# Layer 3's feed-forward block: the parts of a finished sequence move to other places in the software pipeline

## The chip, the cores and the metric

The program runs on one core of a Trainium2 chip. The metric is the device time of one execution in microseconds, the median of several runs. A core has five engines with a queue of instructions each: TensorE (PE; its weight loads are listed apart as PEld), VectorE (DVE), ScalarE (ACT), GpSimd (POOL) and SyncE (SP, which issues transfers). An engine works through its queue in order; semaphores make it wait for the others.

## What is computed

The kernel is a network of four layers, each a feed-forward block, an attention block and the same feed-forward block again, with residuals. The change lies in layer 3's feed-forward block, which is called twice (before and after layer 3's attention). It is itself a small transformer of two inner layers over 4 sequences of 512 tokens, 128 features wide:

```python
def _layer(x, wqkv, qs, ksc, wo, lg, lb, w1, b1, w2, b2):
    h = shift_token(x)                # half of the features come from the token before
    q, k, v = split(h @ wqkv)         # 8 heads of 64
    q, k = rotary_xpos(l2norm(q) * qs, l2norm(k) * ksc)
    o = local_attention(q, k, v)      # windows of 64, each sees itself and the one before
    x = x + o @ wo
    h = shift_token(x)
    h = (h - mean(h)) / sqrt(var(h) + 1e-05) * lg + lb
    a, g = split(h @ w1 + b1)
    return x + (a * gelu(g)) @ w2 + b2
```

Everything is float32.

## The kernel before

`l3_ffn` handles eight **units**: a unit is one inner layer of one sequence, units 0 to 3 are the first inner layer of the four sequences and 4 to 7 the second. A unit is four **steps** of 128 tokens, so a call has 32 steps. `yT` holds the sequences with features on partitions.

The loop over `n` is a software pipeline with a hand-written order. In one turn of the loop it issues six stages, each for another step, in six places:

- place 0, `project` (step n): PE multiplies the shifted tokens by the weights of q and k (`p_qk`) and of v (`pv`). ACT squares q and k (`sq`, line 1737) and copies `v`; DVE multiplies by the rotary tables (`t`, lines 1791 and 1794) and sums the squares (`rn`, 1796); POOL makes the inverse roots of the norms with ten small operations (`ir`, lines 220 to 230), adds the rotary halves (line 1798) and scales k (line 1799). SyncE moves two halves of `v` into `vb`.
- place 1, `to_features` (step n-2): PE transposes q and k (`pt_qk`), ACT copies q (`qT`), DVE copies k (`kT`, line 1823).
- place 2, `exponentials` (step n-4): eight exponentials on ACT with row sums (`s`, line 1737), the reciprocal of the sums on DVE (`sm`, 1860) and the scaling of the weights on POOL (`s<-s,sm`, 1861).
- place 3, `weights` (step n-3): scores on PE (`ps`), mask and maximum on DVE (`s`, 1844; `nm`, 1846 and 1849).
- place 4, `turn_weights` (step n-5): eight transposes of the weights on PE (`pt`), copied by ACT (`PT`).
- place 5, `with_values` (step n-6): PE's products with the values (`po`), copied by DVE (`oT`, line 1887).

When a unit's four steps are through, its feed-forward part is cut into **parts**, and a table `parts` gives each a turn of the loop (counted from the unit's first step) and a place. A part is issued just ahead of the stage in that place:

- `attended` (10, 2): output projection `pz` on PE, the residual sum `yT` on DVE (line 1903), then the shifted copy `h2` (shown as `h` in the profile): ACT copies 64 partitions as they are (line 1740) and DVE the other 64 moved by one token (line 1755)
- `mean` (10, 4): a product with ones gives the mean (`pm`, PE), DVE subtracts it (line 1912), ACT squares the result (`sq2`, shown as `sq<-h`)
- `variance` (11, 0): `pvar` on PE, `rs` on DVE (line 1923), and its inverse root on POOL (lines 214 and 215; 215 is a power)
- `spread` (11, 4): a diagonal of the inverse roots, `dg`, on DVE (line 1931)
- `normed` (12, 0): PE spreads `dg` over the partitions (`pb`), DVE multiplies `h2` by it (line 1941)
- `hidden` 0 (12, 5), 1 and 2 (13, 0): two products each (`pag`), a gelu on ACT (`ge`), and on DVE the product of both (`hh`, line 1954)
- `close_unit` (13, 4): `pz2` on PE, the sum into `yT` on DVE (line 1966)
- `leave` (14, 0), second inner layer only: transposes `pt_z`, the residual, and the output's store or the next normalisation

Three things set the order on the engines. What PE and ACT are given through `mm_in_order`, `transpose_in_order`, `act` and `act_copy` stays in the order in which the program issues it. DVE and POOL are ordered by the scheduler of the framework, by its own estimate. And PSUM has eight banks: three pairs (tag `d`: `p_qk`, `pt_qk`, `ps`, `pt`, `pag`) and two single ones (tag `m`: `pv`, `po`, `pz`, `pm`, `pvar`, `pb`, `pz2`, `pt_z`), each taken in turn, so that a group of products waits until the tile three pairs (or two banks) earlier has been read.

The last unit of a call doesn't go by the table: its parts follow the loop in the list `rest` (in the first call they are spread over the attention that follows).

Of the kernel before, what the change touches and what calls it, by code (L numbers as in the profile page):

```python
# [115 lines left out]
def tile_macaron(ctx, tc, x_in, const_in, vec_in, w0_in, ws_in, ws3_in, w2f_in, w3_in, out):  # L116
# [17 lines left out]
    def bank(tag, name):  # L134
        n = 2 if tag == "d" else 1
        return psum["pool"].tile([P, n * 512], F32, tag=tag, name=name, bufs=psum["bufs"][tag])

    def two_banks(name):

        if "d" in psum["bufs"]:  # L140
            p = bank("d", name)
            return p[:, 0:512], p[:, 512:1024]
        return [bank("e" if "e" in psum["bufs"] else "q", name) for _ in range(2)]
# [3 lines left out]
    for b in range(B):  # L147
        nc.sync.dma_start(x[:, ts(b, TB), :], x_in[:, ts(b, TB), :])
        if b == 0:
            a, z = W0.at["ip"]  # L150
# [24 lines left out]
    yT = keep.tile([P, B, S], F32, name="yT")  # L175
# [8 lines left out]
    def mm_in_order(dst, lhsT, rhs, start=True, stop=True):  # L184
        tc.keep_in_program_order(nc.tensor.matmul(dst, lhsT=lhsT, rhs=rhs, start=start, stop=stop))  # L185

    def transpose_in_order(dst, src):
        tc.keep_in_program_order(transpose(dst, src))
# [107 lines left out]
    def chain(b):  # L296
        parts = deque()
        chains.append([b, clock[0], parts])
        return lambda gap, f, products=True: parts.append((gap, f, products))
# [14 lines left out]
    def leave_normed(b, spare, gap, pinned=False, start=1, to_route=True):  # L314

        st = []
        spare(start, lambda: st.append(statistics(x, b)), False)

        def scale():
            scaled(y, x, b, st[0], pinned)  # L320
            ready.add(b)

        spare(1, scale, False)
        spare(gap, lambda: turn(b))
        if routed and to_route:
            spare(1, lambda: logits(b))
            if b % 2:
                first, second, third = route(b // 2)
                spare(1, first, False)
                spare(routed["gaps"][0], second)  # L330
                spare(routed["gaps"][1], third)
# [1391 lines left out]
    def l3_ffn(w3, tag, first, rb):  # L1723
        with pool(tag) as sb, banks(tag + "ps", d=3, m=2):
            units = [(l, b) for l in range(2) for b in range(B)]
            n_steps = TB * len(units)
            u_state = {}
            s_state = {}

            def W(l, name):  # L1730
                return W3(w3, f"{name}{l}")

            def tmp(name):
                return rb.tile([P, S], F32, tag="tmp", name=name, bufs=4)

            def act(*args, **kw):
                tc.keep_in_program_order(nc.scalar.activation(*args, **kw))  # L1737

            def act_copy(dst, src):
                tc.keep_in_program_order(nc.scalar.copy(dst, src))  # L1740
# [4 lines left out]
            def light(u):  # L1745

                return nc.gpsimd if u else nc.vector

            def shift(dst, src, at=slice(0, S), u=1):

                act_copy(dst[0:64, at], src[0:64, at])
                a = max(at.start, 1)
                if at.start == 0:
                    light(u).memset(dst[64:128, 0:1], 0.0)
                nc.vector.tensor_copy(dst[64:128, a : at.stop], src[64:128, a - 1 : at.stop - 1])
# [134 lines left out]

            whole = slice(0, S)

            def attended(u, at=whole):
                l, b = units[u]
                oT = u_state[u]["oT"]
                n = at.stop - at.start
                pz = bank("m", "pz")
                for fc in range(4):
                    mm_in_order(
                        pz[:, :n], W(l, "wo").rearrange("p (c n) -> p c n", n=D)[:, fc, :], oT[:, fc, at], fc == 0, fc == 3  # L1900
                    )
                z = yT[:, b, :]
                nc.vector.tensor_add(z[:, at], pz[:, :n], z[:, at])
                if at.start == 0:
                    u_state[u]["h2"] = rb.tile([P, S], F32, tag="h2", name="h2", bufs=2)
                shift(u_state[u]["h2"], z, at)

            def mean(u, at=whole):
                h2, n = u_state[u]["h2"], at.stop - at.start
                pm = bank("m", "pm")  # L1910
                mm_in_order(pm[:, :n], onesm, h2[:, at])
                nc.vector.tensor_sub(h2[:, at], h2[:, at], pm[:, :n])
                sq = u_state[u]["sq", at.start] = tmp("sq2")
                act(sq[:, :n], h2[:, at], AF.Square)

            def variance(u, at=whole):

                sq, n = u_state[u].pop(("sq", at.start)), (at.stop - at.start) // P
                pv = bank("m", "pvar")
                for t in range(n):  # L1920
                    mm_in_order(pv[:, 2 * t : 2 * t + 2], sq[:, ts(t, P)], onesm[:, 0:2])
                rs = u_state[u]["rs", at.start] = rb.tile([P, TB], F32, tag="rs", name="rs", bufs=2)
                nc.vector.tensor_copy(rs[:, :n], pv[:, : 2 * n].rearrange("p (t i) -> p t i", i=2)[:, :, 0])
                eng = nc.vector if u == len(units) - 1 else nc.gpsimd
                inverse_root(rb, rs[:, :n], rs[:, :n], f"ir{n}", ALU.add, 1e-5, eng)
# [17 lines left out]
            def hidden(u, c, at=whole):  # L1943
                l, b = units[u]
                a, n = HCH[c]
                h2, w1, m = u_state[u]["h2"][:, at], W(l, "w1"), at.stop - at.start
                if c == 0 and at.start == 0:
                    u_state[u]["hh"] = rb.tile([P, 3, S], F32, tag="hh", name="hh")
                pg, pa = two_banks("pag")
                mm_in_order(pg[:n, :m], w1[:, HID + a : HID + a + n], h2)  # L1950
                mm_in_order(pa[:n, :m], w1[:, a : a + n], h2)
                ge = tmp("ge")
                act(ge[:n, :m], pg[:n, :m], AF.Gelu, bias=W(l, "b1g")[:n, c : c + 1])
                nc.vector.scalar_tensor_tensor(
                    u_state[u]["hh"][:n, c, at], pa[:n, :m], W(l, "b1a")[:n, c : c + 1], ge[:n, :m], ALU.add, ALU.mult
                )
# [13 lines left out]
            def leave(b, at=whole):  # L1970
                pt = bank("m", "pt_z")
                t0, n = at.start // P, (at.stop - at.start) // P
                for t in range(n):
                    transpose_in_order(pt[:, ts(t, P)], yT[:, b, ts(t0 + t, P)])
                tiles = slice(b * TB + t0, b * TB + t0 + n)
                xb = x[:, tiles, :].rearrange("p t d -> p (t d)")
                nc.vector.scalar_tensor_tensor(xb, pt[:, : n * P], 0.5, xb, ALU.mult, ALU.add)
                if first:
                    leave_normed(b, chain(b), 3)
                else:  # L1980
                    nc.sync.dma_start(out[:, tiles, :], x[:, tiles, :])
# [17 lines left out]
            if first:  # L1999
                scale_layer(0)  # L2000

            parts = [
                (attended, 10, 2), (mean, 10, 4), (variance, 11, 0), (spread, 11, 4), (normed, 12, 0),
                (lambda u: hidden(u, 0), 12, 5), (lambda u: hidden(u, 1), 13, 0), (lambda u: hidden(u, 2), 13, 0),
                (close_unit, 13, 4), (lambda u: leave(units[u][1]) if units[u][0] else None, 14, 0),
            ]
            later, last = {}, len(units) - 1
            for u in range(len(units)):
# [6 lines left out]
            for n in range(-2, n_steps + 6):  # L2015
                for place, (part, lag) in enumerate((
# [6 lines left out]
                    tick()  # L2023
            assert not later, later
            rest = [attended, mean, variance, spread, normed]
            rest += [lambda u, at, c=c: hidden(u, c, at) for c in range(3)] + [close_unit, lambda u, at: leave(units[u][1], at)]
            if first:
# [13 lines left out]
    with pool("ws") as wp:  # L2041
# [9 lines left out]
        with pool("l2x") as l2x:  # L2051
# [58 lines left out]
            with pool("l2g") as sb, banks("l2gps", a=2, g=2, t=2, m=2):  # L2110
# [7 lines left out]
                while slots:  # L2118
                    n = slots[0][0]
                    run_to(slots, n)  # L2120
                    at = (n - SLOTS - 1) * part
# [12 lines left out]
    with pool("l3r") as rb:  # L2134
        l3_ffn(w3, "l3f", True, rb)
        l3_attn()
        l3_ffn(w3, "l3g", False, rb)
# [145 lines left out]
```

## Time and profile before

| | us |
|---|---|
| median of 3 runs | 2669.72 (2664.33 to 2672.69) |
| profiled execution | 2684.83 |
| its span | 2683.0 |
| first call of `l3_ffn`, loop | about 1529.7 to 1935 |
| second call of `l3_ffn` | about 2264 to 2683 |

| engine | busy us | share of the span |
|---|---|---|
| PE | 2274.4 | 85% |
| DVE | 1776.3 | 66% |
| ACT | 1306.2 | 49% |
| POOL | 951.7 | 35% |

Shares over the whole span mix many stages; the change is judged within the two calls. Three views serve there. The table of windows gives the busy time of each engine in a stretch, with the clock that PE was granted (1.00 is full speed). The table of waits adds up an engine's idle time by the instruction that waited and the one that released it. The timeline lists instructions in order of time, with the idle time of the engine ahead of each. A step can be cut out of the timeline by `sq<-p_qk`, ACT's square of the projections, which comes once in each step.

### The profile page before, as it was taken

What the parts mean: (1) busy time and instruction counts of PE and PEld (TensorE: products, weight loads), DVE (VectorE), ACT (ScalarE), POOL (GpSimd) and SP (SyncE); (2) the same over time, 40 slices, a digit from 0 to 9 for tenths busy, and PEclk for the clock granted to TensorE, in tenths of its full rate; (3) what the DMA queues carried; (4) which work ended last, traced back from release to release, by engine and by line L of the source; (5) the groups of instructions that cost most, each with busy time, mean ns of one, the idle gap of its engine ahead of it and who ended that gap; (6) DMA issues with size and microseconds to landing.
All of it is one profiled execution on the core that took longest, in us unless ns stands there. A gap on an engine that the chain in (4) does not pass through costs nothing.

```text
span 2683.0 us, 50819 instructions
## 1 busy us (share of the span) xinstructions
PE 2274.4 (85%) x19070; PEld 1288.0 (48%) x19070; DVE 1776.3 (66%) x4790; ACT 1306.2 (49%) x3159; POOL 951.7 (35%) x1532
## 2 busy tenths in 40 slices
PE   6578589988679989988787778998899998799988
PEld 2255244443344434477567645555433333555555
DVE  3745667775676777565554488777567775877774
ACT  3056125443333544343443357776525554677773
POOL 2023023232232233214331377766310001876761
PEclk8789799998889999789778879999989999899998
DMA  3052000000000000246145701010000000110100
GB/s 146 8 175 73 0 1 2 1 1 1 1 1 1 1 5 1 84 146 216 32 139 160 246 23 23 21 23 19 1 1 1 1 1 9 27 23 19 23 21 13
DMA packets 40142, 113.21 MB, mean 42 GB/s; under 512 B 7064, under 2 KB 16536, under 8 KB 39384
## 3 DMA queue, kind: packets, MB, share of 16 engines
q1 hardware_dynamic: 36520, 100.94, 11.8%
q0 software_dynamic: 2944, 6.04, 1.1%
q8 instruction: 151, 2.47, 0.4%
q10 hardware_dynamic: 432, 2.98, 0.3%
q14 instruction: 95, 0.78, 0.1%
HBM read 79.78 MB, written 15.47 MB: 35 GB/s over the span
## 4 chain that ended last, share of the span: by engine, by line
PE 56%; DVE 21%; ACT 8%; POOL 8%; issue 5%; DMA 1%; another core or an unknown queue 0%; POOLq 0%; DVEq 0%; SPq 0%; ACTq 0%
PE pk_at L185 10%; PE po_at L185 6%; PE pa L185 4%; PE pq_at L185 4%; PE pag L185 4%; PE po L185 3%; ACT s L1737 3%; PE pg L185 2%; PE pe L185 2%; PE p_qk L185 2%; DVE t L1794 2%; DVE t L1791 2%; PE pz L185 2%; PE idle L185 2%; PE pt L182 2%
## 5 line engine op out<-in xcount | busy, mean ns | idle before, releaser
L894 ACT ACTIVATE PT<-pk_at 128x512 f32<-128x512 f32 (+3 forms) x768 | 335.3, 488 | 401.2 <-PE pq_at L185 254.0
L185 PE MATMUL pk_at<-qx,km 32*128 32x512 f32 (+3 forms) x1536 | 401.4, 555 | 5.9 <-ACT PT L894 2.7
L866 DVE CUSTOM_DVE_ANT_0 s<-pq_at,cst 128x384 f32<-128x384 f32 (+3 forms) x512 | 249.9, 488 | 99.0 <-PE pq_at L185 44.8
L185 PE MATMUL pq_at<-km,qT 32*128 32x128 f32 (+3 forms) x1024 | 275.8, 504 | 18.3 <-DVE nm L866 14.4
L1737 ACT ACTIVATE s<-s,nm,rn 128x128 f32<-128x128 f32 x512 | 245.5, 482 | 3.2 <-DVE nm L1849 3.0
L897 POOL TENSOR_SCALAR_AFFINE_SELECT PT<-PT 128x256 f32<-128x256 f32 x256 | 104.5, 410 | 381.7 <-ACT PT L894 381.6
L185 PEld LDWEIGHTS pk_at<-qx,km 32*128 32x128 f32 x1536 | 147.1, 190 | 154.3 <-issue 93.5
L185 PE MATMUL po_at<-PT,vh 128*32 128x128 f32 (+3 forms) x2432 | 205.6, 395 | 8.7 <-POOL PT L897 6.9
L868 DVE TENSOR_REDUCE nm<-pq_at 128x1 f32<-128x512 f32 x256 | 165.4, 685 | 55.3 <-PE pq_at L185 53.8
L1798 POOL TENSOR_TENSOR t<-t,t 128x1024 f32<-128x1024 f32 x64 | 151.2, 2362 | 109.7 <-DVE t L1794 105.1
L215 POOL TENSOR_TENSOR ln_r<-ir,minus_half 128x4 f32<-128x4 f32 x60 | 62.0, 1034 | 351.5 <-DVE ir L214 349.5
L185 PE MATMUL pq_at<-km,t 32*128 32x512 f32 x512 | 170.9, 661 | 0.7 <-DVE nm L868 0.4
L185 PE MATMUL p_qk<-w,hT 128*128 128x512 f32 x256 | 142.4, 684 | 15.6 <-DVE t L1794 9.6
L1861 POOL TENSOR_TENSOR s<-s,sm 128x1024 f32<-128x1024 f32 x64 | 121.3, 1896 | 52.1 <-DVE sm L1860 44.1
L185 PEld LDWEIGHTS po_at<-PT,vh 128*32 128x32 f32 x2432 | 54.4, 109 | 174.4 <-issue 128.5
L182 PE MATMUL pt<-ident,s 128*128 128x128 f32 x640 | 94.0, 295 | 48.5 <-POOL s L1861 32.0
L185 PEld LDWEIGHTS pq_at<-km,qT 32*128 32x128 f32 x1024 | 110.6, 191 | 48.9 <-DVE nm L866 28.9
L1419 POOL DMA_INDIRECT xg<-yd,come x60 | 57.5, 958 | 180.3 <-PE pt_x L182 72.3
L289 ACT COPY yT<-pt_y 128x512 f32<-128x512 f32 x56 | 32.7, 584 | 180.0 <-PE pt_y L182 179.5
L1737 ACT ACTIVATE sq<-p_qk 128x1024 f32<-128x1024 f32 x64 | 65.5, 1023 | 109.8 <-PE p_qk L185 61.6
L182 PEld LDWEIGHTS pt<-ident,s 128*128 128x128 f32 x640 | 79.0, 151 | 81.1 <-POOL s L1861 44.2
L1791 DVE TENSOR_TENSOR t<-p_qk,w 128x1024 f32<-128x1024 f32 x64 | 78.3, 1223 | 58.5 <-ACT sq L1737 53.0
(457 smaller groups left out, 5374.7 us busy)
## 6 DMA issues: line engine op xcount, KB each, us to landing
wf<-in_w2f_dram SPq DMA_DIRECT2D x45, 836.0 KB
vb<-v SPq DMA_DIRECT2D x112, 128.0 KB
w<-in_w2f_dram SPq DMA_DIRECT2D x15, 836.0 KB
skew<-qe SPq DMA_DIRECT2D x16, 512.0 KB
rel<-skew SPq DMA_DIRECT2D x64, 128.0 KB
od<-o SPq DMA_DIRECT2D x60, 64.0 KB
w<-in_w_dram SPq DMA_DIRECT2D x1, 3200.0 KB
w<-in_w_dram SPq DMA_DIRECT2D x12, 173.0 KB
```

Source lines behind the costliest of these rows:

```text
L182: return nc.tensor.transpose(dst, src, ident[: src.shape[0], : src.shape[0]])
L185: tc.keep_in_program_order(nc.tensor.matmul(dst, lhsT=lhsT, rhs=rhs, start=start, stop=stop))
L215: nc.gpsimd.tensor_tensor(dst, v, minus_half[:, :n], ALU.pow)
L866: nc.vector.tensor_tensor_reduce(s[:, :nk], pq[:, :nk], causal[:, S - nk :], 1.0, -BIG, ALU.add, ALU.max, to)
L868: nc.vector.tensor_reduce(to, pq, AX.X, ALU.max)
L894: by_order(nc.scalar.activation(PT[:, i, q0:], pk[:, q0:], AF.Exp, scale=SC8))
L897: nc.gpsimd.affine_select(d, d, pattern=[[0, 2], [1, P]], base=0, channel_multiplier=-1, compare_op=ALU.is_ge, fill=0.0)
L1419: nc.gpsimd.indirect_dma_start(xT[s], None, yds[k][:, :], bass.IndirectOffsetOnAxis(ap=come[:, i : i + 1], axis=0))
L1737: tc.keep_in_program_order(nc.scalar.activation(*args, **kw))
L1791: nc.vector.tensor_mul(by_head(t1), by_head(p3), over(tab[:, 0]))
L1798: nc.gpsimd.tensor_add(t1, t1, t2)
L1861: nc.gpsimd.tensor_mul(s, s, bcast(sm, P))
```

## The change

Two parts are split into their halves and the table of places is rewritten. `attended` becomes `summed` (`pz` and the residual sum) and `shifted` (the shifted copy); `mean` becomes `centred` (`pm` and the subtraction) and `squared` (`sq2`). The joint functions stay for the list `rest`. No operation is added or taken away.

```diff
-            def attended(u, at=whole):
+            def summed(u, at=whole):
...
                 z = yT[:, b, :]
                 nc.vector.tensor_add(z[:, at], pz[:, :n], z[:, at])
+
+            def shifted(u, at=whole):
                 if at.start == 0:
                     u_state[u]["h2"] = rb.tile([P, S], F32, tag="h2", name="h2", bufs=2)
-                shift(u_state[u]["h2"], z, at)
-
-            def mean(u, at=whole):
+                shift(u_state[u]["h2"], yT[:, units[u][1], :], at)
+
+            def attended(u, at=whole):
+                summed(u, at)
+                shifted(u, at)
+
+            def centred(u, at=whole):
                 h2, n = u_state[u]["h2"], at.stop - at.start
                 pm = bank("m", "pm")
                 mm_in_order(pm[:, :n], onesm, h2[:, at])
                 nc.vector.tensor_sub(h2[:, at], h2[:, at], pm[:, :n])
+
+            def squared(u, at=whole):
+                h2, n = u_state[u]["h2"], at.stop - at.start
                 sq = u_state[u]["sq", at.start] = tmp("sq2")
                 act(sq[:, :n], h2[:, at], AF.Square)
+
+            def mean(u, at=whole):
+                centred(u, at)
+                squared(u, at)
...
             parts = [
-                (attended, 10, 2), (mean, 10, 4), (variance, 11, 0), (spread, 11, 4), (normed, 12, 0),
-                (lambda u: hidden(u, 0), 12, 5), (lambda u: hidden(u, 1), 13, 0), (lambda u: hidden(u, 2), 13, 0),
-                (close_unit, 13, 4), (lambda u: leave(units[u][1]) if units[u][0] else None, 14, 0),
+                (summed, 10, 2), (shifted, 10, 3), (centred, 11, 1), (squared, 11, 3), (variance, 12, 0), (spread, 12, 2),
+                (normed, 12, 4), (lambda u: hidden(u, 0), 13, 0), (lambda u: hidden(u, 1), 13, 1),
+                (lambda u: hidden(u, 2), 13, 1), (close_unit, 13, 5),
+                (lambda u: leave(units[u][1]) if units[u][0] else None, 14, 1),
             ]
```

So the residual sum stays at (10, 2); the shifted copy goes behind the exponentials of that turn; the mean's product goes from (10, 4) to (11, 1), the squares from (10, 4) to behind the exponentials of turn 11, the variance from (11, 0) to (12, 0), `spread` from (11, 4) to (12, 2), `normed` from (12, 0) to (12, 4), the first `hidden` from (12, 5) to (13, 0), the other two from ahead of the projections of turn 13 to behind them, and `close_unit` and `leave` one place later. In the instruction streams this also moves POOL's part of the variance: before it stands behind the scaling of weights of turn 10 and ahead of the additions of turn 11, afterwards behind the scaling of turn 11 and ahead of the additions of turn 12; and DVE's `dg` stands ahead of the multiplications of turn 12 (`t`, line 1791) where it stood ahead of those of turn 11. In the changed file the lines are: subtraction 1918, `rs` 1936, `dg` 1944, `normed` 1954, `hh` 1967, sum of `close_unit` 1979.

## The prediction

> **What bounds the kernel now.** I read the page's shares first: TensorE is busy for 85% of the span and the chain that ended last is PE for 56%, so the question is where PE idles in the layer-3 FFN and for whom. The two calls run from 1529.7 and from 2264 us. I call a unit's four loop steps (its first step plus 10, 11, 12, 13) A, B, C, D, and show the third unit of the first call. Its steps, cut at the start of the square of the projections (`sq<-p_qk`, ACT), in the table of windows (window, its us, then busy us with instructions of PE, PEld, DVE, ACT, POOL, granted clock, DMA share, GB/s):
>
> ```profile
> 1715.60:1729.39 13.79, 12.12 (x105) 7.41 (x104) 9.31 (x14) 8.47 (x23) 11.68 (x19) 1.00 0.09 20
> 1729.39:1738.02 8.63, 7.74 (x89) 5.06 (x88) 8.26 (x12) 6.81 (x20) 4.55 (x12) 1.00 0.07 15
> 1738.02:1751.78 13.76, 12.28 (x99) 6.78 (x98) 9.95 (x14) 10.15 (x24) 11.01 (x18) 1.00 0.09 20
> 1751.78:1761.20 9.42, 9.42 (x93) 5.86 (x92) 8.29 (x12) 8.20 (x21) 4.89 (x12) 1.00 0.14 32
> 1715.60:1761.20 45.60, 41.56 (x383) 25.11 (x382) 35.81 (x51) 33.62 (x88) 32.13 (x59) 1.00 0.10 22
> ```
>
> PE works 41.6 of 45.6 us; at most 4 us a unit are to be had. The table of waits of PE in that unit (us in total, times, longest) says for whom:
>
> ```profile
> PE pvar L185 <- ACT sq L1737: 1.3, 1, 1.3
> PE pt L182 <- POOL s L1861: 1.1, 1, 1.1
> PE pt L182 <- DVE t L1794: 0.9, 1, 0.9
> PE pag L185 <- DVE kT L1823: 0.4, 1, 0.4
> PE pm L185 <- ACT h L1740: 0.4, 1, 0.4
> ```
>
> The rows behind the change, from the timeline (start, duration, engine, line, operation; in brackets the engine's idle time before it and who ended it):
>
> ```profile
> 1721.45 0.62 ACT L1740 COPY h<-yT 64x512 f32<-64x512 f32 x1 [3.58 <-DVE yT L1903]
> ...
> 1726.25 1.90 POOL L1861 TENSOR_TENSOR s<-s,sm 128x1024 f32<-128x1024 f32 x1
> ...
> 1728.55 1.04 POOL L215 TENSOR_TENSOR rs<-ir,minus_half 128x4 f32<-128x4 f32 x1
> 1729.62 0.69 DVE L1931 SCALAR_TENSOR_TENSOR dg<-ident,rs 128x512 f32<-128x512 f32 x1 [1.89 <-POOL rs L215]
> 1730.45 1.22 DVE L1791 TENSOR_TENSOR t<-p_qk,w 128x1024 f32<-128x1024 f32 x1
> ...
> 1733.01 2.37 POOL L1798 TENSOR_TENSOR t<-t,t 128x1024 f32<-128x1024 f32 x1 [2.58 <-DVE t L1794]
> ...
> 1739.83 1.90 POOL L1861 TENSOR_TENSOR s<-s,sm 128x1024 f32<-128x1024 f32 x1
> ```
>
> In A, ACT stands 3.58 us before the shift copy `h`, with A's eight exponentials behind it, and `sq2` and PE's `pvar` behind those. That is what the change attacks. The second point is `dg`: DVE waits 1.89 us for POOL, which takes `rs` up only after the scaling of a step's weights (`s<-s,sm`). Today this is free: `dg` ends at 1730.31 and the next multiplication could not start before 1730.45.
>
> **The change, walked through one unit.** In the changed instruction streams the units 0 to 4 of both calls (ten) have one order on every engine, so one walk serves. Zero is PE's start of A's `p_qk` (1713.52 in the trace). PE's advance from one group to the next, from the timeline: `p_qk` 1.73 (1.83 in A), `pv` 0.86, `pt_qk` 0.96 (0.88 in A), `pz` 3.53, `ps` 1.03, `pt` 0.97, `po` 1.08, `pm` 0.9, `pvar` 0.92, `pb` 0.96, `pag` 1.91 and 3.54 for the other two, `pz2` 2.69.
>
> A: `pm` and `pvar` leave, nothing holds PE. `pz` 3.57, `ps` 7.10, `pt` 8.13, `po` 9.10, B's `p_qk` at 10.2. Before: 13.9. Gain **3.7**. ACT runs the exponentials at once (4.4 to 8.3) and the copy of 0.62 behind them ends at 8.9; its user `pm` comes at 12.8, so the copy is covered by 3.9 us. DVE's half of the copy (0.42) stays where it was.
>
> B: PE gets `pm` and ends `po` at 17.9. `pvar` needs `sq2`, which still stands behind a step's exponentials, now B's. In the trace they end 8.07 after the step's `p_qk` starts (1736.05 to 1744.12); with `pm` 0.9 ahead of them that is 19.1, with `sq2` 19.7. PE waits 1.9 (today 1.27), and C's `p_qk` queues behind it and starts at 20.7. Before: 22.5. Still 1.8 ahead.
>
> C is where I see it lost. POOL takes B's `t` sum 5.62 after B's `p_qk` (1727.39 to 1733.01): 15.8. From that to the scaling of weights it is 6.82 (1733.01 to 1739.83, all POOL work without a gap): 22.6. From the scaling's start to the end of `rs` 3.34 (1726.25 to 1729.59): **26.0**. `rs` cannot be earlier, since in POOL's stream it stands behind B's scaling. DVE has `dg` ahead of C's multiplications, so it idles some 4.7 us and C's `t` starts at 26.75 where it could at 20.7 + 3.05 = 23.7. Queued behind `dg` are `t`, `rn`, `kT`, `s`, `nm`, and only then `normed`. Who waits: PE is at `pb` at 25.3 and gets `dg` at 26.7 (1.4); at `pt` at 27.7 and gets its PSUM pair, which `t` frees, 2.57 after `t` starts, 29.3 (1.6); after `po` it stands at 31.4 before `pag`, now D's first work. `normed` (0.74) follows `nm`, whose end is 6.53 after `t`'s start (1730.45 to 1736.98): 34.0. PE waits **2.7**. Today `pag` comes 5 us after `normed`.
>
> D: `pag` 34.05, `p_qk` 36.0, the other two `pag` at 38.6, `pt_qk` 42.1, `ps` 43.05 (0.15 for `hh`, freed by DVE behind `t` and `rn`), `pt` 44.3, `pz2` 45.2, `po` 47.9, next `p_qk` **49.0**. The split gelus load the exponential table once per unit as before, so no table load is added.
>
> So a unit goes from 45.6 to 49.0, +3.4; by PE's waits 1.9 + 1.4 + 1.6 + 2.7 + 0.15 = 7.75 against 4.04, +3.7. I take **3.55**.
>
> Clock: after the `pvar` wait of only 1.27 us some units show this:
>
> ```profile
> 1727.39 1.97 PE L185 MATMUL p_qk<-w,hT 128*128 128x512 f32 x4
> ...
> 1818.58 3.52 PE L185 MATMUL p_qk<-w,hT 128*128 128x512 f32 x4
> ```
>
> The granted clock is 0.64 over 1817.60 to 1822.14. The ten units average 46.27 between the marks, 0.67 over the undisturbed one, partly for this. One such stretch costs 3.52 - 1.97 = 1.6, with its remainder 1.7. Stretches before C's end hide in waits for others; one at `pag` does not. Bounds: the old 0.67 goes (-0.65 a unit), or every unit pays a full one (+1.7). I take three units in four, 1.3 - 0.65 = **+0.65**, since the longer waits of the trace (2.99, 3.07, 3.29, 3.30 us) were all followed by slow matmuls. The Trainium skill's "TensorE: Matmul & The Clock Gate" (Part 1) says that the clock falls after an idle window of about 3.4 us; none of the new waits is that long, so by that rule no clock is lost and the sum below would be 6.5 us smaller. The row above, after a 1.27 us wait, speaks against so long a limit, and I go by the row.
>
> Units 5 and 6 of each call run while steps drain. There `pt` waits 3.0 to 3.3 us for POOL's scaling (2607.78, 2644.52, 1886.72, 1921.56), as the exponentials stood late behind `h`. With them earlier I estimate per call 0 to -6: `pvar` and `dg` become the limit in place of the scaling, worth about 3 in the last of the four places (`pag` at 2643.1 by the same steps, against 2645.99) and little elsewhere. I take -3 a call, **-6**. The last unit uses the old joint parts. `leave` starts a place later; in the second call its store goes behind two `vb` transfers on the sync queue, and nothing but the end waits for it: 0.
>
> Sum: 10 x (3.55 + 0.65) - 6 = **+36 us**. The bounds are 10 x (3.4 - 0.65) - 12 = +15 and 10 x (3.7 + 1.7) = +54. The profiled execution took 2684.8 us (span 2683.0), 15 over the median of 2669.7; I add the same microseconds to both: 2721 profiled, **2706** as the median (2685 to 2724).
>
> **Rivals.** *POOL in time (about no change).* If `rs` came 3.0 us earlier, so that `dg` ends by 23.7, C's `t` is not held, the unit is 49.0 - 3.05 = 45.95, ten give +3.5, with the drain -6: 2667, between 2661 and 2673. For it: POOL's spans are rough. Against: 6.82 us of gapless POOL work ahead of the scaling.
>
> *The gain of A is kept (faster).* Place: `normed`, for which `pag` waits. If it is done when C's `po` is (28.4, by the unheld PE) instead of 34.0, only `pvar`'s wait is left: 41.6 + 1.9 = 43.5, -2.1 a unit, with the drain -27: 2643. It decides from 5.6 us earlier; 3.0 of them need `dg` in time and the other 2.6 that DVE does C's base work faster than the 6.5 us the trace shows. Against: `normed` stands behind `nm` in the stream.
>
> *Cold at every wait (slower still).* Two stretches of 1.7 a unit not hidden, no drain gain: 10 x (3.7 + 3.4) = +71, 2741. For it: four waits within 16 us; against: two of them lie ahead of another engine's limit.
>
> That the copy does not move is no case: in the changed streams it stands behind the eight exponentials on ACT.
>
> **Numbers.** Forecast 0.68, POOL in time 0.10, gain kept 0.08, cold 0.14. The range goes from the forecast's lower bound, 2685, up into the cold case, 2738, which leaves out both upper rivals and a little of the cold one, 0.2. A measurement of this kernel tells some 0.3% (8 us) from no change: faster 0.08 and 0.02 of POOL in time, 0.10; same 0.08; slower 0.82.
>
> **What would show it.** ACT's 3.58 us before `h` gone and A at 10 us between marks (10.2, 10.5, 15.3, 13.0 for A to D); `dg` with 4 to 5 us of idle DVE before it; new PE waits on `dg` and on DVE's `h` before `pag`, of 1.4 and 2.7. If A shortens and C stays at 13.8, the step of POOL's queue is wrong; if C is above 16, the clock. If A does not shorten, the first step is.

## The result, and the profile after

The changed kernel takes 2714.34 us (median of 4 runs, 2711.68 to 2714.51), the kernel before 2670.95 in runs on the same chip: a ratio of 1.0165, 95% interval 1.0150 to 1.0180, slower by 43 us. The profiled execution took 2714.47 us, its span is 2712.8.

The table of windows, cut as before, for the third unit of the second call (columns as for the kernel before; the last column but two is the granted clock):

```profile
2459.82:2470.06 10.24, 10.24 (x95) 6.13 (x94) 10.05 (x14) 7.95 (x22) 5.68 (x13) 1.00 0.12 27
2470.06:2480.56 10.50, 8.66 (x97) 5.99 (x96) 7.90 (x12) 7.33 (x22) 8.31 (x17) 1.00 0.07 15
2480.56:2495.68 15.12, 11.14 (x93) 7.08 (x92) 9.24 (x13) 8.89 (x23) 10.65 (x17) 0.89 0.08 18
2495.68:2508.78 13.10, 12.87 (x101) 7.13 (x100) 10.13 (x13) 9.55 (x23) 7.42 (x13) 1.00 0.10 21
2459.82:2508.78 48.96, 42.91 (x383) 26.33 (x382) 37.32 (x52) 33.72 (x88) 32.07 (x59) 0.97 0.09 20
```

The number of instructions is the same (PE 383). A fell from 13.8 to 10.2: the wait of ACT for the shift copy is out of the chain. The copy now stands behind the exponentials and starts without a wait, where ACT stood 3.58 us before it:

```profile
2465.82 0.61 ACT L1740 COPY h<-yT 64x512 f32<-64x512 f32 x1
```

B, C and D (1.9, 1.4 and 3.7 us longer) give the gain back and 3.4 us more. PE's table of waits in this unit says where:

```profile
PE pvar L185 <- ACT sq L1737: 1.7, 1, 1.7
PE pb L185 <- DVE dg L1944: 1.6, 1, 1.6
PE pt L182 <- DVE t L1794: 1.2, 1, 1.2
PE pag L185 <- DVE nm L1849: 1.2, 1, 1.2
```

The timeline of POOL and DVE shows whom `dg` waits for:

```profile
2480.63 1.89 POOL L1861 TENSOR_TENSOR s<-s,sm 128x1024 f32<-128x1024 f32 x1
2482.60 0.23 POOL L214 TENSOR_SCALAR ir<-rs 128x4 f32<-128x4 f32 x1
2482.91 1.04 POOL L215 TENSOR_TENSOR rs<-ir,minus_half 128x4 f32<-128x4 f32 x1
2483.98 0.69 DVE L1944 SCALAR_TENSOR_TENSOR dg<-ident,rs 128x512 f32<-128x512 f32 x1 [4.91 <-POOL rs L215]
2484.59 1.22 DVE L1791 TENSOR_TENSOR t<-p_qk,w 128x1024 f32<-128x1024 f32 x1
...
2491.03 0.74 DVE L1954 SCALAR_TENSOR_TENSOR h<-h,w,pb 128x512 f32<-128x512 f32 x1
```

DVE stands idle for 4.91 us where it was 1.89, and C's multiplication `t` starts the moment `dg` is out of the way. So `dg` now holds up DVE, which before it didn't.

Not every unit is alike. Five of the ten take 48.9 to 49.1 us and five 50.6, and the second kind has this in PE's timeline (the fourth unit of the second call; in the third the same projection took 1.97):

```profile
2526.54 1.05 PE L185 MATMUL pvar<-onesm,sq 128*128 128x2 f32 x8 [1.75 <-ACT sq L1737]
2527.45 3.33 PE L185 MATMUL p_qk<-w,hT 128*128 128x512 f32 x4
...
2540.87 3.09 PE L185 MATMUL pag<-h,w 128*128 128x512 f32 x4 [2.62 <-DVE nm L1849]
```

Two stretches with slow matmuls, each shortly behind a wait. The first is hidden, because C then waits less for `dg`; the second, at `pag`, is not. A unit without a slow stretch that lengthens it is called undisturbed below.

Where the time came from, by the marks (the starts of `sq<-p_qk`) in the two profiled executions:

| stretch | before | after | difference |
|---|---|---|---|
| up to the first call's first step (code that the change does not touch) | 1534.1 | 1521.2 | -12.9 |
| first ten steps, both calls | 169.0 | 165.3 | -3.8 |
| ten units, both calls | 462.7 | 498.0 | **+35.3** |
| from step 30 of the first call to the second call: drain, then layer 3's attention | 415.2 | 425.5 | +10.4 |
| from step 30 of the second call to the end | 102.0 | 102.8 | +0.8 |

Without the first row the sum is +42.7, against 43.4 by the medians. The first row is left out because the profiled execution of before was 13.9 us over its median (2684.83 against 2670.95), which is about what it lost there.

### The profile page after: what moved, and what is told of

It is laid out like the page before. It is cut to its first block, busy times and chain, and to the rows that moved or that the text cites. A ratio compares the mean times of both kernels' runs of the same rounds, so it can differ in the third digit from the quotient of the medians.

```text
span 2712.8 us, 50905 instructions
## 1 busy us (share of the span) xinstructions
PE 2283.0 (84%) x19070; PEld 1291.4 (48%) x19070; DVE 1786.0 (66%) x4790; ACT 1307.1 (48%) x3159; POOL 952.1 (35%) x1532
## 4 chain that ended last, share of the span: by engine, by line
PE 56%; DVE 20%; POOL 11%; ACT 5%; issue 4%; DMA 3%; SPq 0%; POOLq 0%; DVEq 0%; ACTq 0%
PE pk_at L185 10%; PE po_at L185 5%; PE pq_at L185 4%; PE pa L185 4%; PE p_qk L185 3%; PE pz L185 3%; PE po L185 3%; PE pag L185 2%; PE idle L185 2%; PE pe L185 2%; PE pg L185 2%; DVE t L1794 2%; POOL t L1798 2%; PE pv L185 2%; DVE t L1791 2%
## 5 line engine op out<-in xcount | busy, mean ns | idle before, releaser
L185 PE MATMUL p_qk<-w,hT 128*128 128x512 f32 x256 | 147.9, 706 | 15.5 <-DVE t L1794 9.4
L185 PEld LDWEIGHTS pq_at<-km,qT 32*128 32x128 f32 x1024 | 110.1, 190 | 48.9 <-DVE nm L866 28.9
L185 PE MATMUL pag<-h,w 128*128 128x512 f32 (+3 forms) x204 | 97.9, 625 | 23.3 <-DVE nm L1849 23.3
```

## The experiments

Theory: `dg` stands behind POOL's scaling of a step's weights, holds DVE and with it C, and `pag` waits ahead of the projections; the gain of A is used up there. Rivals: the shift alone would bring the gain (S); the later places of `hidden` are the loss (H). Ratios are to the kernel before, run on the same chip beside each experiment; that kernel's own median was 2671 to 2674 us beside the changed kernel and eight of the experiments, and 2687 to 2689 beside the last four (e12, e13, e15, e16), so ratios are compared and not times.

**Half the table, twice.** One kernel takes the old table and moves only the shifted copy, the other only the `hidden` parts and `close_unit`.

```diff
 e1_shift_only, against before:
-                (attended, 10, 2), (mean, 10, 4), (variance, 11, 0), (spread, 11, 4), (normed, 12, 0),
+                (summed, 10, 2), (shifted, 10, 3), (mean, 10, 4), (variance, 11, 0), (spread, 11, 4), (normed, 12, 0),
 e6_hidden_only, against before:
-                (lambda u: hidden(u, 0), 12, 5), (lambda u: hidden(u, 1), 13, 0), (lambda u: hidden(u, 2), 13, 0),
-                (close_unit, 13, 4), (lambda u: leave(units[u][1]) if units[u][0] else None, 14, 0),
+                (lambda u: hidden(u, 0), 13, 0), (lambda u: hidden(u, 1), 13, 1), (lambda u: hidden(u, 2), 13, 1),
+                (close_unit, 13, 5), (lambda u: leave(units[u][1]) if units[u][0] else None, 14, 1),
```

> Only the shifted copy moves behind the exponentials (10, 3); mean, variance, spread, normed, hidden and close_unit keep their old places. POOL theory: A's 3.58 us on ACT goes, but dg is then limited by POOL (scaling of A's weights ends at 14.3, rs 16.0, dg 16.7 after A's p_qk) and holds B's multiplications by 0.9 us, so pt of B comes at 19.3 where it came at 19.5: the unit stays at about 45.4 us instead of 45.6 and the whole at 2664 to 2674 us against 2671 of before, with a PE wait of about 1.9 us at pt for DVE's t. Rival (the ACT wait is a cost by itself, and only the later mean and variance lose it): about 42 a unit, 10 x 3.6 us off, 2635 us.

> Only the feed-forward products move (the first hidden to 13, 0, the other two to 13, 1, close_unit 13, 5, leave 14, 1); the shifted copy, mean, variance, spread and normed keep their old places. POOL theory: normed is long done when the first pag is reached, so nothing waits; the unit is 45.3 us, the whole 2662 to 2675 us against 2671 of before. Rival (the split of the products around D's projections is what costs): a unit of 48 to 49 and 2700 to 2710 us.

Measured: 0.9984 (0.9969 to 0.9999) and 0.9980 (0.9968 to 0.9991), undisturbed units of 45.39 and 45.18 us. Both rivals fall. The shift alone takes 1.2 us out of A and puts 1.0 into B (12.6, 9.6, 13.8, 9.4): with `pm` and `pvar` still in A's turn, PE now waits 1.9 us at `pt` of B for DVE's `t`, as was expected. The places of `hidden` alone cost nothing as long as `normed` is early. So the loss is in the places of the mean and the variance, or in what the edits do together.

**The first hidden chunk behind the projections.** PE then has 2.6 us of work ahead of `pag` while DVE finishes `normed`.

```diff
-                (normed, 12, 4), (lambda u: hidden(u, 0), 13, 0), (lambda u: hidden(u, 1), 13, 1),
+                (normed, 12, 4), (lambda u: hidden(u, 0), 13, 1), (lambda u: hidden(u, 1), 13, 1),
```

> The changed kernel, with the first hidden at (13, 1) too, behind D's projections (2.6 us of products). POOL theory: the wait before pag (2.7 us) is covered by the projections, the waits at pvar, pb and pt stay: a unit of 46.4 us, the whole 2678 to 2692 us. Rival (the split of the products around D's projections costs, the more the later they come): no gain, 2710 us or more.

Measured: 1.0029 (1.0015 to 1.0043), median 2680.95, undisturbed units of 46.88 (mean 46.98). The wait at `pag` is gone (0.6 is left, at `pv`), and the slow matmuls that followed it too; PE still waits 1.6 at `pb` and 1.2 at `pt`. Of the loss per unit 2 us, and nearly all of the low clock that was not hidden, come from this one place in the table.

**The root of the variance off POOL's queue.** If POOL's queue is the reason for the late `dg`, the root on DVE (the function's other branch, Newton steps) should free C.

```diff
-                inverse_root(rb, rs[:, :n], rs[:, :n], f"ir{n}", ALU.add, 1e-5, eng)
+                if u == len(units) - 1:
+                    inverse_root(rb, rs[:, :n], rs[:, :n], f"ir{n}", ALU.add, 1e-5, eng)
+                else:
+                    inverse_root(rb, rs[:, :n], rs[:, :n], f"ir{n}s", ALU.add, 1e-5, nc.vector, True)
...
-                (summed, 10, 2), (shifted, 10, 3), (centred, 11, 1), (squared, 11, 3), (variance, 12, 0), (spread, 12, 2),
+                (summed, 10, 2), (shifted, 10, 3), (centred, 11, 1), (squared, 11, 3), (variance, 12, 0), (spread, 12, 0),
```

(`dg`, `t` and `rn` are also pinned to the program's order, so that DVE takes the root and `dg` ahead of C's `t`.)

> The changed kernel, with the inverse root of the variance on DVE (eight small operations) instead of POOL, and dg ahead of C's multiplications as in the changed kernel (order pinned). The queue of POOL is gone from the path of dg. POOL theory: dg ends by 23.2 after A's p_qk, C's multiplications start at 23.7, the waits at pb and at pt go, the one before pag stays at 2.6: the unit is 46.0 us instead of 49.0 (or 50.7 cold), the whole 2670 to 2685 us against 2714 of the changed kernel. Rival (the order of the products in D costs): the unit stays above 48 and the whole above 2700 us.

Measured: 1.0171 (1.0141 to 1.0201), units of 49.8 in the mean. A miss, by 29 us at the least. In the timeline of this kernel, DVE and POOL together:

```profile
2475.87 3.23 DVE L221 TENSOR_SCALAR ir4s<-ir4s 128x4 int32<-128x4 int32 x1
...
2477.18 1.89 POOL L1861 TENSOR_TENSOR s<-s,sm 128x1024 f32<-128x1024 f32 x1
```

An instruction over 128x4 numbers took 3.23 us, where it takes 0.17 with POOL idle, and ended at 2479.10, 0.03 after the scaling. So DVE does not wait for POOL by a semaphore here, but inside an instruction, for the same scaling. In six of the ten units it is this instruction that stands so long (3.23 to 3.24 us), in the other four the one ahead of it (2.97 to 3.34). The experiment had measured the same wait by another way.

**Another form of the same instructions.** Scalar_tensor_tensor with constant tiles in place of the two tensor_scalar instructions and of the copy; once in the changed table, once with `hidden` behind the projections.

```diff
+                    stt(xx, var, 1.0, eps_t[:, :n], ALU.mult, ALU.add)
+                    stt(yy.bitcast(I32), xx.bitcast(I32), -0.5, magic_t[:, :n], ALU.mult, ALU.add)
+                    for to, a, b in ((yy, -0.703952253, 1.681913895), (rs[:, :n], -0.50000016, 1.50000048)):
+                        nc.vector.tensor_mul(t, yy, yy)
+                        stt(t, t, a, xx, ALU.mult, ALU.mult)
+                        stt(to, t, b, yy, ALU.add, ALU.mult)
```

> The root of the variance on DVE again, but in the two-tensor form alone: scalar_tensor_tensor with constant tiles takes the place of the two tensor_scalar instructions and of the copy; as many DVE instructions as in e2_root_on_dve less one, the same places and pins. Theory of the port: in e2 the two tensor_scalar instructions stood blocked until POOL's gapless work ended, so e2 measured the same wait by another way; without them dg ends ahead of C's first multiplication, the waits of PE at pb, pt and pag go, the unit is 45.5 to 46.5 and the time 2670 to 2685. Rival, POOL's queue was never the cause (or any DVE instruction on such small tiles waits for POOL): units stay at 49 to 50.6 and the time at 2708 to 2720.

> The root on DVE as in e9_root_stt and the first hidden chunk behind the projections as in e3_hidden_behind. e3's unit of 46.9 holds waits of PE of 1.7 for sq2, 1.6 at pb, 1.2 at pt and 0.6 at pv. If POOL's queue causes the two in the middle, they go and the gain of step A is kept: unit 43.5 to 45, time 2645 to 2662, below both kernels. If DVE's own work ahead of normed is the limit, the unit stays at 46.5 to 47 and the time at 2675 to 2685.

Measured: 1.0114 (1.0095 to 1.0134) and 1.0032 (1.0018 to 1.0045), undisturbed units of 48.34 and 46.25. Both missed; the second came out in its rival's range of time (2680.92 us, 2675 to 2685). In the timeline of the first:

```profile
2383.93 2.29 DVE L1952 SCALAR_TENSOR_TENSOR irt<-irt 128x4 f32<-128x4 f32 x1
2384.30 1.89 POOL L1865 TENSOR_TENSOR s<-s,sm 128x1024 f32<-128x1024 f32 x1
2386.24 0.16 DVE L1953 SCALAR_TENSOR_TENSOR irt<-irt 128x4 f32<-128x4 f32 x1
```

Again it ends (2386.22) when POOL's scaling does (2386.19). The form is not what counts. The instruction ahead of these, which reads `pvar` from PSUM, took 0.16 us in all 14 cases, 13 of them beside a busy POOL; the ones with both operands in SBUF up to 2.29. That gave the next test.

**One operand in PSUM.** The same chain with its scratch, and `rs`, in the bank of `pvar`.

```diff
+                    x, yp, tp, rs = (pv[:, i * 16 : i * 16 + n] for i in range(1, 5))
+                    stt(x, var, 1.0, eps_t[:, :n], ALU.mult, ALU.add)
+                    for to in (y, yp):
+                        stt(to.bitcast(I32), x.bitcast(I32), -0.5, magic_t[:, :n], ALU.mult, ALU.add)
+                    for outs, a, b in (((yp, y), -0.703952253, 1.681913895), ((rs,), -0.50000016, 1.50000048)):
+                        nc.vector.tensor_mul(t, y, yp)
+                        stt(tp, t, a, x, ALU.mult, ALU.mult)
+                        for to in outs:
+                            stt(to, tp, b, y, ALU.add, ALU.mult)
```

> As e9_root_stt, but every small DVE instruction of the root reads one operand from PSUM (its scratch, and rs itself, lie in the bank of pvar; two results are written twice for that, so DVE gets two instructions more), and dg reads rs from there. In e9 the small instructions with both operands in SBUF took up to 2.29 us where the same took 0.16 with POOL idle, and each ended when POOL's gapless stretch did. Theory of the port: with an operand in PSUM they run beside POOL, dg ends some 2.4 us earlier than in e9, C's first multiplication is not held, the unit is 45.9 to 47.6 and the time 2670 to 2690. That would be the test of POOL's queue that e2 and e9 failed to be. Rival, the small instructions wait for POOL wherever their operands lie, or DVE's multiplications are not what C waits for: units 48.3 to 50, time 2700 to 2715.

Measured: 1.0072 (1.0056 to 1.0089). In the timeline of DVE and POOL (POOL works without a pause from 2381.57 to the end of its scaling, 2384.93):

```profile
2382.78 0.17 DVE L1956 SCALAR_TENSOR_TENSOR pvar<-irt,pvar 128x4 f32<-128x4 f32 x1
2382.98 0.17 DVE L1958 SCALAR_TENSOR_TENSOR pvar<-pvar,irt 128x4 f32<-128x4 f32 x1
2383.04 1.89 POOL L1865 TENSOR_TENSOR s<-s,sm 128x1024 f32<-128x1024 f32 x1
2383.18 0.69 DVE L1964 SCALAR_TENSOR_TENSOR dg<-ident,pvar 128x512 f32<-128x512 f32 x1
2384.02 1.22 DVE L1795 TENSOR_TENSOR t<-p_qk,w 128x1024 f32<-128x1024 f32 x1
```

No instruction of the chain is long any more, `dg` included, and `t` starts 0.15 after `dg` has ended because the squares come then, not because of `dg`. The waits at `pb` and `pt` are gone, `pag` still waits 2.4. The undisturbed unit is 45.79: 3.2 below the changed kernel's, and 2.55 below that of e9_root_stt, which has the same order and differs in where the operands of the root lie (and two more small instructions). So the wait behind POOL's work is what held C. The mean of the ten is 47.6: one is undisturbed, seven have one slow stretch and two have two. The ratio stands for 2690 at the earlier baseline, the upper end of what was expected; the 2706.69 us as measured lie in the rival's range, but beside a kernel before of 2687.44.

**Both cures together**, and the same with the old table in units 5 and 6, whose parts run while the pipeline drains.

```diff
 e15_psum_hidden_drain_old, against e13_psum_hidden:
-            parts = [
+            new_parts = [
...
+                parts = new_parts if u < 5 else old_parts
```

> As e10_root_stt_hidden_behind, with the root of e12_root_psum. e10 kept waits of PE of 1.0 at pb and 1.2 at pt for dg and for the multiplications behind it. Theory of the port and of POOL's queue: they go, and the unit is 43.3 to 44.8, the time 2642 to 2664, below both kernels. Rival: the unit stays at 46.2 and the time at 2676 to 2684.

> e13_psum_hidden with the old timetable (and the root on DVE) for units 5 and 6. In e5_drain_old the old places made the way to the first attention product 2.7 shorter than in the changed kernel, which the whole time did not show. If that holds here, the time is 1 to 5 below e13; if the drain does not depend on the places once the root is off POOL, it is equal to e13 within 2.

Measured: 1.0011 (0.9997 to 1.0024) and 0.9934 (0.9915 to 0.9952). The undisturbed unit is 43.7 in both, as expected, and the gain of A is kept; but the ten units average 45.5 and 45.6, with lengths of 43.7, 45.4 and 47.1 to 47.8. The time of e13 was missed for that, and it is no faster than the kernel before. In e13, PE behind the one wait that is left:

```profile
1780.14 1.62 PE L189 MATMUL pvar<-onesm,sq 128*128 128x2 f32 x8 [1.75 <-ACT sq L1741]
1781.62 3.76 PE L189 MATMUL p_qk<-w,hT 128*128 128x512 f32 x4
```

The old places in units 5 and 6 brought more than expected: by the marks 5.2 us between step 30 of the first call and the second call, 6.3 from step 30 of the second call to the end, and 17.6 by the medians (some 6 us of that are not in the profiled executions).

**The drain alone**: the changed kernel with the old table in units 5 and 6 (the same edit).

> The new timetable for units 0 to 4, the old one for units 5 and 6 of each call. My term for the drain was -6, the trace shows about +11, nearly all of it between the end of the first call's steps and the second call. If those 11 us belong to the new places of units 5 and 6, the time is 2701 to 2707 with the ten units unchanged at 49.8. If they come from the state in which the steps arrive (or from the attention between the calls), it stays at 2711 to 2717.

Measured: 1.0156 (1.0138 to 1.0174), the same as the changed kernel. By the marks the way to the second call is 3.1 us shorter, 2.7 of it ahead of the first product of the attention, and the ten units are 1.7 longer in the sum through one more slow stretch. So the new places of units 5 and 6 hold some 3 of the 11 us, and a whole time cannot tell that.

**Idle products against the low clock**, first in the changed kernel in the wait for `h` ahead of `pag`:

```diff
                 pg, pa = two_banks("pag")
+                for _ in range(2 if c == 0 and u < len(units) - 1 else 0):
+                    mm_in_order(pg, onesm, cst[:, :S])
```

> The changed kernel with two idle 128x512 products put ahead of the first hidden chunk in the PSUM bank that the chunk then overwrites, in the wait for DVE's h; output unchanged. The units of the changed kernel have two lengths, 48.9 and 50.65. If the 1.7 between them is a stretch at a low granted clock that starts in this wait, most units come out at 48.9 and the time is 2702 to 2709. If the cold stretch belongs to another wait, the lengths stay and the time is 2712 to 2722 (the products themselves end ahead of h, and cost nothing).

Measured: 1.0140 (1.0123 to 1.0157), 2709.81, just above the expected range. No unit of 50.6 is left; the ten are 48.9 to 49.5, mean 49.17 against 49.80, in all 6.3 us. By the ratios it is 6.7 us, though the two intervals overlap. Step B is still 1.4 to 2.4 longer in six of the ten units, and C shorter for it: the slow stretch behind `pvar` is hidden as before.

Then, in the best kernel so far, in the wait ahead of `pvar`:

```diff
                 pv = bank("m", "pvar")
+                for _ in range(2 if u < len(units) - 1 else 0):
+                    mm_in_order(pv, onesm, cst[:, :S])
```

> e15_psum_hidden_drain_old with two idle 128x512 products (0.87 us each by pm) put ahead of pvar into its PSUM bank, which pvar then overwrites; output unchanged. They fill PE's remaining wait of 1.74 us for sq2. In e13 and e15 the units have the lengths 43.7, 45.4 and 47.1 with a mean of 45.5, and the longer ones show the projection right behind this wait at a low granted clock (3.76 us instead of 1.99). If this wait starts the stretch, nearly all ten units come out at 43.7 to 44.2, some 17 us less in all: a ratio of 0.985 to 0.990 to the kernel before, against 0.993 for e15. If the stretch is due to the clock's own period or to other waits, the lengths stay mixed and the ratio is 0.991 to 0.996.

Measured: **0.9884** (0.9865 to 0.9904), 2656.23 beside 2688.64 us. In PE's timeline of the third unit of the second call the wait is filled (the first line holds both idle products), and the projection runs at full speed:

```profile
2448.11 1.99 PE L189 MATMUL pvar<-cst,onesm 128*128 128x512 f32 x4
2449.94 1.05 PE L189 MATMUL pvar<-onesm,sq 128*128 128x2 f32 x8
2450.85 1.97 PE L189 MATMUL p_qk<-w,hT 128*128 128x512 f32 x4
```

All ten units are 43.9, to within 0.03, as this one:

```profile
2432.18:2476.08 43.90, 43.20 (x387) 25.64 (x386) 37.79 (x60) 33.73 (x88) 30.99 (x57) 1.00 0.11 23
```

So the wait of 1.74 us at `pvar` was what started the slow stretches (the last section says why only some units had them). This version beats both kernels.

## Why the prediction was right, point by point

The forecast was 2706, within 2685 to 2738, and slower at 0.82; measured 2714. The steady units came as forecast; the term for the drain had the wrong sign.

- **A: right.** 10.2 was the forecast from `p_qk` to `p_qk` and 10.23 came.
- **B: right.** A wait of 1.9 at `pvar` was forecast, 1.75 measured; C's `p_qk` at 20.7, measured 20.74 (2478.49 after 2457.75, in the unit shown).
- **C, POOL's queue: right, and shown by experiment.** `rs` ends at 26.2 (forecast 26.0), DVE idles 4.91 (4.7), `t` starts at 26.84 (26.75), `normed` ends at 34.0 (34.0). With `dg` out of POOL's way the unit is 45.79; the rival *POOL in time* had computed 45.95 for that case. So the rival's arithmetic held, and its condition did not.
- **The unit: right.** 48.96 against 49.0, +3.4 over the undisturbed 45.6, in steps of 10.2, 10.5, 15.1 and 13.1 (forecast 10.2, 10.5, 15.3, 13.0). The wait at `pag` was smaller (1.16 for 2.7) where slow matmuls ahead of it had already filled the time, and 2.62 where not; the end of `normed`, which sets it, was the same.
- **Clock: right in kind, too large in size.** I took +0.65 a unit net. The changed units average 49.80, 0.87 over the undisturbed 48.93, and the old 0.67 fell away: +0.20. One unit in two paid, not three in four. Only the stretch at `pag` counts, and which units have it follows from where they fall on the clock's grid of 3.41 us (last section): those that start 0.75 to 1.60 us behind a grid line paid, those at 0.19 to 0.50 and at 2.50 to 3.02 did not. The prediction took the share from the longer waits of the trace alone. That the stretches follow waits well below 2 us was the row against the rule of the Trainium skill ("TensorE: Matmul & The Clock Gate", Part 1, an idle window of about 3.4 us). The runs go with the row: filling a wait of 1.74 us removed every slow stretch from the ten units. The same section says that the window runs freely; the traces agree, since the grid stands fixed from the start of an execution to its end, whatever the kernel does.
- **The first ten steps** were not in the sum: -3.8.
- **The drain: wrong.** The sum took -6 for units 5 and 6, on the reasoning that exponentials which come earlier let the scaling and with it `pt` come earlier. The step that failed is "`pvar` and `dg` become the limit in place of the scaling, worth about 3": they became the limit, but nothing was won by it. Between the start of unit 6's `pz` and that of its `pz2` in the first call, PE waits 6.1 us (2.46 at `pvar` for `sq2`, 2.86 at `pb` for `dg`, 0.7 at `pm`), where it waited 5.4 before. `pb` and `pt` behind that take 2.05 and 1.92 instead of about 1, and `pz2` comes 1.5 us later, counted from `pz`. From step 30 to the first product of the attention it is +5.2; in the second call, from step 30 to the end, +0.8. Which of the new places costs this is not shown: the old table in units 5 and 6 takes 2.7 us off the way to the attention, but e3_hidden_behind, which moves only the first hidden chunk of all units, takes off 2.9.
- **Not settled:** the other 5.2 us of the first call's stretch lie in layer 3's attention, whose code is unchanged. From its first to its last row maximum the profiled executions take 281.1 to 286.7 us (282.9 before, 286.6 in the changed kernel), and kernels with the same table of places stand near both ends (281.05 with the root on DVE, 286.08 with its other form). I cannot say whether this belongs to the change.

So the steady part, +35.3, is nearly the whole +36; it was mis-sized by -6.7 (the clock and its bounds) and the rest, drain and first steps, by +13. Errors of both signs met: that the total came within 9 us is luck to that extent.

Among the rivals, *the gain of A is kept* put its decision at `normed` and computed 43.5. e13 reached 43.7: `dg` in time gave 3.2 us, and PE's work put ahead of `pag` the other 2.1.

## What to carry to other kernels

A part that is moved to cover one engine's wait takes its whole chain with it: look up where each of its instructions then stands in every other queue, GpSimd's above all, and what stands behind it there. Try the edits of a table singly: here two of them alone were harmless, the whole table cost 1.6%, and with repairs of its new waits it gains 1.2%. A wait of TensorE of less than 2 us that nothing can remove may still be worth filling with idle products: here it started windows at half clock that cost 1.7 us each.

## What the hardware did that I had not expected

**Small DVE instructions can stand for as long as POOL works without a pause.** In e9 each group of DVE instructions can be sorted by whether POOL was busy. Line 1952, with both operands in SBUF: 0.15 to 0.17 us in the 20 cases beside an idle POOL, and 2.28 to 2.29 in the eight beside a busy one. Line 1948, with an operand in PSUM: 0.15 to 0.16 in the 13 cases beside a busy POOL. The reductions `rn` over 1024 numbers from SBUF, with a single operand: 1.20 to 1.21 in all 64, all beside a busy POOL. Copies from SBUF to SBUF suffer too: of the 16 shifted copies of 64x511 into `hT`, eight start in the changed kernel while POOL scales the weights, end 0.28 us after it and take 1.61 us instead of 0.42 (16.9 us for all 16, 7.9 before). The Trainium skill, "SBUF — State Buffer" (Who interferes with whom), has the rule: DVE and GpSimd share one pair of ports under an exclusive lock, and DVE takes it for copies and tensor_scalar in their fast modes and for two SBUF operands. The trace agrees, and adds one thing: with POOL's work back to back the DVE instruction of e2 did not get in between two of its instructions, but stood 3.23 us, over a part of the scaling of k, the `vb` memset and the scaling of the weights. In e9 that is not so throughout: the instruction ahead of the long one shown took 0.92 us and ended at 2383.89, 0.02 after the scaling of k. POOL's spans are rough, so the runs leave open what decides this.

**The slow stretches of TensorE come in whole windows of 3.41 us.** In every trace of this case the granted clock is either 1.00 or 0.50, and it changes only on a grid of 3.41 us (a value such as 0.89 is the mean of a longer stretch). Around the `pvar` wait shown above for e13, window by window (columns as before):

```profile
1777.00:1780.40 3.40, 1.65 (x38) 1.35 (x36) 3.35 (x6) 3.40 (x14) 2.90 (x7) 1.00 0.00 0
1780.42:1783.82 3.40, 3.40 (x10) 2.35 (x11) 2.86 (x14) 0.56 (x1) 2.99 (x8) 0.50 0.00 0
1783.84:1787.24 3.40, 3.40 (x6) 1.26 (x5) 1.22 (x2) 1.14 (x2) 1.24 (x1) 0.50 0.00 0
1787.26:1790.66 3.40, 3.40 (x48) 2.54 (x47) 3.40 (x5) 2.96 (x11) 1.63 (x1) 1.00 0.20 43
```

The wait lies in the first window, and the next two run at half clock. Half of 3.41 us is 1.7, and that is what one slow window adds to a unit when nothing hides it (45.40 less 43.72 in e13; the unit with these two windows takes 47.09). That this is about as much as the wait itself is chance. Which units are hit goes by where they fall on the grid: of the 20 units of e13 and e15, those that start 1.05 to 2.09 us behind a grid line take 45.4 us, those at 2.14 to 2.48 take 47.1 to 47.8, and those at 2.70 to 3.10 take 43.7. Six of the ten units of e16 start at 1.09 to 2.23 and still take 43.9, so it was the idle products that removed the slow windows, and not a better place on the grid. How much idle time a window has to hold for the next to be slow, the runs do not settle.
